# Layer 1 of a two-layer graph network with keys on partitions: eight accumulators, one exponential, row maxima by a fused instruction during layer 0

## The chip, the core and the metric

The kernel runs on one core of a Trainium2 chip. The metric is the device time of one execution in microseconds (us); each kernel is given as the median of its runs. A ratio is the mean time of one kernel's fast runs over that of the other's of the same rounds, so it is not quite the ratio of the medians quoted beside it.

In the profile PE is TensorE's matmul stream, PEld its weight loads, DVE is VectorE, ACT ScalarE, POOL GpSimd, SP the engine that issues DMAs. The granted clock is the share of its full clock that TensorE was given. L300 is line 300 of that kernel's file; the numbers shift between kernels, so I name tiles too.

## The reference, cut to what matters

```python
# x: (8, 2048, 256), adj: (2048, 2048) of 0 and 1, the same for all 8 batches
h = maximum(layernorm(x), 0)                     # layer 0: 4 heads, softmax per chunk of 256 keys
...                                              # scores clipped to +-10, masked, times v, projected,
x = x + layernorm(ctx @ Wo.T + bo + h) * gamma + beta
h = maximum(layernorm(x), 0) @ W                 # layer 1
e = leaky_relu((h @ a1)[:, :, None] + (h @ a2)[:, None, :], 0.01)
e = where(adj == 0, -1e9, e)
x = x + maximum(softmax(e) @ h, 0)               # over all 2048 keys
```

The logit of layer 1 is a function of a sum of two numbers, one of the query ("src", from a1) and one of the key ("dst", from a2).

## The kernel before

Eight batches one after the other. In layer 0 a batch has four blocks of 512 queries; each block has 16 passes (logits, mask, exponential, mix) for two heads and one chunk of keys, then a serial tail: output projection, two layer norms, and the start of layer 1.

The matmuls of this kernel write to PSUM (PE ps_s<-q,k and the like in the traces). I count it in tiles of 128x512 fp32 and call one a bank. The kernel uses eight of them, shared out as three rotating pools, each of two buffers:

```python
ps_s: [P, 2, 512]   # two banks each: logits of layer 0, transposes of layer 1
ps_a: [P, 512]      # mixes, accumulators of layer 1
ps_m: [P, 512]      # all small products and transposes
```

The start of layer 1 for a block, and layer 1 with queries on partitions:

```python
def start_layer1(x4, nb, sd):
    _, rn = norm_stats(x4)
    hT = normed_transposed(x4, rn)
    for t2 in range(TB // 2):
        pp = ps_m()
        ...  # matmul(pp, hT, w1s): layer 1's projection
        nc.scalar.activation(g[...], pp..., AF.Copy)
        ...  # four fused multiply-and-sum instructions on VectorE: src and dst into sd

def layer1(pool, b, xs, sd):
    ...  # dst spread over all partitions
    for t in range(NT):                                     # 16 tiles of queries
        nc.vector.scalar_tensor_tensor(d, sign[:, t, :], BIG, dst, op0=ALU.mult, op1=ALU.min)
        nc.vector.tensor_reduce(dmax, d, AX.X, ALU.max)     # both 128x2048
        ...
        for half in range(2):
            nc.scalar.activation(e1, d[:, cols], AF.Exp, bias=b1)
            nc.scalar.activation(e2, d[:, cols], AF.Exp, bias=b2, scale=SLOPE)
            nc.vector.tensor_tensor(e1, e1, e2, op=ALU.max)
            ...  # 8 transposes into ps_s, two evacuations, 8 matmuls into one accumulator
```

## Time and profile before

| | before |
|---|---|
| time | 5757.45 us (5756.26 to 5758.06, 3 runs) |
| layer 0 of a batch | 523.3 us |
| ends of layer 1's projection, from one block to the next | 116.3, 116.2, 104.1 us |
| layer 1 of a batch | 186.7 us |
| mean granted TensorE clock | 0.922 |

I use the same landmarks for every kernel. Layer 0 of a batch runs from the start of its first q projection to the end of layer 1's projection in its fourth block; layer 1 from there to the next batch's first q projection. They are read from TensorE's order of time, and are medians over the eight batches.

The windows of the first batch show the same stages (start and end; then length, and the busy time of PE, PEld, DVE, ACT and POOL, each with its count; then the granted clock, the DMA share and GB/s):

```profile
75.60:262.20 186.60, 184.57 (x970) 127.67 (x970) 88.61 (x180) 67.10 (x83) 37.03 (x43) 0.93 0.00 1
262.20:378.50 116.30, 114.55 (x691) 85.99 (x692) 67.01 (x142) 40.97 (x46) 32.12 (x37) 0.90 0.00 1
494.60:598.70 104.10, 84.76 (x563) 65.67 (x563) 56.98 (x133) 32.63 (x37) 30.22 (x34) 0.89 0.00 1
598.70:785.40 186.70, 152.38 (x793) 127.53 (x791) 152.24 (x231) 90.44 (x108) 20.08 (x19) 0.96 0.06 20
```

In the second block TensorE is busy 114.55 of 116.30 us, and in layer 1 TensorE and VectorE are busy 152 us each of 187.

### The profile page before, as it was taken

The numbers are of one execution on the slowest core, as the hardware profiler recorded it, in microseconds if no ns is written. First come the engines' busy times: TensorE is split into PE (matmuls) and PEld (weight loads), VectorE is DVE, ScalarE is ACT, GpSimd is POOL, SyncE is SP. The second block draws the span as 40 slices with busy tenths as digits, with TensorE's granted clock in tenths as the row PEclk, the third lists the DMA queues.
The fourth block names the chain that finished last, engine by engine and source line by source line (L and its number), as shares of the span: only waits on it lengthen the run. The fifth ranks groups of instructions, "written<-read, shape, count | busy, mean of one in ns | idle before, by whom it ended". The sixth has DMA issues, their size and how long they took to land.

```text
span 5753.9 us, 73951 instructions
## 1 busy us (share of the span) xinstructions
PE 5208.2 (91%) x29840; PEld 3939.6 (68%) x29840; DVE 3477.6 (60%) x6501; ACT 2191.4 (38%) x2545; POOL 1228.1 (21%) x1369
## 2 busy tenths in 40 slices
PE   7999799987999889998899978999789997899978
PEld 4777667766677666776667757676576776767767
DVE  4555755558455584555845558455584555845567
ACT  3333443334433344333533335433353333533334
POOL 2222102231022301223112221123211232112221
PEclk7999899999999899998999989999899988999889
DMA  4000000000000000000000000000000000000000
GB/s 150 1 1 1 15 15 1 1 1 15 15 1 1 1 15 15 1 1 1 19 11 1 1 1 23 8 1 1 1 23 8 1 1 1 23 4 1 1 1 15
DMA packets 39203, 57.16 MB, mean 10 GB/s; under 512 B 2000, under 2 KB 36816, under 8 KB 36816
## 3 DMA queue, kind: packets, MB, share of 16 engines
q1 hardware_dynamic: 38864, 52.44, 2.8%
q8 instruction: 238, 3.90, 0.3%
q14 instruction: 101, 0.83, 0.0%
HBM read 35.65 MB, written 16.78 MB: 9 GB/s over the span
## 4 chain that ended last, share of the span: by engine, by line
PE 74%; DVE 14%; POOL 6%; ACT 4%; issue 2%; DMA 0%; POOLq 0%; SPq 0%; ACTq 0%; DVEq 0%
PE ps_a L238 32%; PE ps_s L219 17%; PE ps_a L352 10%; PE ps_m L194 4%; DVE d L328 3%; PE ps_m L300 3%; DVE e L343 2%; DVE st L331 2%; PE ps_m L203 2%; PE ps_m L183 2%; PE ps_s L346 2%; POOL o L282 1%; DVE e L224 1%; PE ps_m L271 1%; ACT e L341 1%
## 5 line engine op out<-in xcount | busy, mean ns | idle before, releaser
L238 PEld LDWEIGHTS ps_a<-v,e 128*128 128x128 f32 x16384 | 1994.8, 202 | 357.8 <-issue 321.4
L238 PE MATMUL ps_a<-v,e 128*128 128x65 f32 x16384 | 2061.0, 287 | 0.0
L228 ACT ACTIVATE e<-e 128x1024 f32<-128x1024 f32 x1024 | 1081.8, 1056 | 1682.4 <-DVE e L224 1650.2
L224 DVE SCALAR_TENSOR_TENSOR e<-ps_s,bound 128x1024 f32<-128x1024 f32 x1024 | 1213.4, 1217 | 273.4 <-PE ps_s L219 273.2
L219 PE MATMUL ps_s<-q,k 64*128 64x512 f32 x4096 | 1211.3, 638 | 66.3 <-DVE e L224 66.3
L252 POOL TENSOR_TENSOR ctx<-ctx,part 128x256 f32<-128x256 f32 x896 | 648.0, 723 | 2698.9 <-DVE part L251 2698.9
L352 PE MATMUL ps_a<-g,eT 128*128 128x257 f32 x4096 | 952.9, 385 | 66.9 <-ACT eT L348 45.9
L352 PEld LDWEIGHTS ps_a<-g,eT 128*128 128x128 f32 x4096 | 756.7, 190 | 214.0 <-ACT eT L348 83.5
L219 PEld LDWEIGHTS ps_s<-q,k 64*128 64x128 f32 x4096 | 389.6, 190 | 391.2 <-issue 148.8
L243 DVE RECIPROCAL rz<-ps_a 128x4 f32<-128x4 f32 x1024 | 182.7, 180 | 783.3 <-PE ps_a L238 783.3
L346 PE MATMUL ps_s<-ident,e 128*128 128x128 f32 x2048 | 288.0, 282 | 180.7 <-DVE e L343 179.8
L251 DVE TENSOR_TENSOR part<-ps_a,rz 128x256 f32<-128x256 f32 x896 | 379.6, 424 | 88.5 <-DVE rz L243 1.4
L360 POOL TENSOR_TENSOR x<-x,r 128x256 f32<-128x256 f32 x128 | 136.3, 1065 | 1254.8 <-DVE st L332 511.9
L346 PEld LDWEIGHTS ps_s<-ident,e 128*128 128x128 f32 x2048 | 247.4, 145 | 221.7 <-DVE e L343 114.4
L348 ACT ACTIVATE eT<-ps_s 128x512 f32<-128x512 f32 x256 | 150.6, 590 | 615.8 <-PE ps_s L346 575.2
L343 DVE TENSOR_TENSOR e<-e,e 128x1024 f32<-128x1024 f32 x256 | 310.1, 1217 | 79.3 <-ACT e L342 79.3
L341 ACT ACTIVATE e<-d,st 128x1024 f32<-128x1024 f32 x256 | 291.2, 1137 | 112.8 <-DVE st L334 112.8
L328 DVE SCALAR_TENSOR_TENSOR d<-sign,dst 128x2048 f32<-128x2048 int8 x128 | 312.7, 2448 | 9.6 <-ACT dst L324 9.6
L342 ACT ACTIVATE e<-d,st 128x1024 f32<-128x1024 f32 x256 | 291.1, 1137 | 0.0
L331 DVE TENSOR_REDUCE st<-d 128x1 f32<-128x2048 f32 x128 | 290.5, 2274 | 0.0
L183 PE MATMUL ps_m<-ident,hn 128*128 128x128 f32 x512 | 121.0, 368 | 165.7 <-ACT hn L173 165.2
L183 PEld LDWEIGHTS ps_m<-ident,hn 128*128 128x128 f32 x512 | 67.2, 175 | 288.8 <-ACT hn L173 237.5
(71 smaller groups left out, 3130.3 us busy)
## 6 DMA issues: line engine op xcount, KB each, us to landing
rows<-in_adj_dram SPq DMA_DIRECT2D x16, 1024.0 KB, 5.0
x<-in_x_dram SPq DMA_DIRECT2D x32, 512.0 KB, 3.8
out_dram<-x SPq DMA_DIRECT2D x32, 512.0 KB, 2.9
raw<-in_L_gnn_Wq_dram SPq DMA_DIRECT2D x1, 256.0 KB, 4.7
raw<-in_L_gnn_Wk_dram SPq DMA_DIRECT2D x1, 256.0 KB, 4.9
raw<-in_L_gnn_Wv_dram SPq DMA_DIRECT2D x1, 256.0 KB, 5.3
raw<-in_L_gnn_Wo_dram SPq DMA_DIRECT2D x1, 256.0 KB, 5.1
w1s<-in_L_gnn_W_dram SPq DMA_DIRECT2D x1, 256.0 KB, 6.4
```

The lines of the kernel that those rows point to most:

```text
L219: nc.tensor.matmul(s[:, i, :], k[p][i * DH:(i + 1) * DH, mt * P:(mt + 1) * P], q[p][i * DH:(i + 1) * DH, cols], start=True, stop=True,)
L224: nc.vector.scalar_tensor_tensor(e, s, -CLIP * SC, bound[:, mt, cols][:, None, :].to_broadcast([P, 2, NB]), op0=ALU.max, op1=ALU.min,)
L228: nc.scalar.activation(e, e, AF.Exp, scale=1.0 / SC)
L238: nc.tensor.matmul(a[:, s, :], es[kt][:, i, t * P:(t + 1) * P], v[:, j * KT + kt, 2 * p + i, :], start=kt == 0, stop=kt == KT - 1,)
L251: nc.vector.tensor_tensor(part, num, rzb, op=ALU.mult)
L252: nc.gpsimd.tensor_tensor(dst, dst, part, op=ALU.add)
L328: nc.vector.scalar_tensor_tensor(d, sign[:, t, :], BIG, dst, op0=ALU.mult, op1=ALU.min)
L331: nc.vector.tensor_reduce(dmax, d, AX.X, ALU.max)
L341: nc.scalar.activation(e1, d[:, cols], AF.Exp, bias=b1)
L343: nc.vector.tensor_tensor(e1, e1, e2, op=ALU.max)
L346: nc.tensor.transpose(pt[:, k * P:(k + 1) * P], e1[:, k * P:(k + 1) * P], ident)
L352: nc.tensor.matmul(acc, eT[:, k * P:(k + 1) * P], g[:, m, :], start=m == 0, stop=m == NT - 1)
```

## The change

Its intent: in layer 1 keys go on partitions, so the exponentials are already in the layout that the matmul wants. The transposes and their evacuations fall away. The logit is rewritten so that one exponential does for two: with low = 0.01 dst and high = dst - low, leaky(src + dst) = Relu(0.99 src + high) + 0.01 src + low. The row's stabilising maximum needs the largest dst of a row's neighbours; that is computed block by block in layer 0 by a fused add-and-max on VectorE. All eight of these banks become accumulators for half of the queries at once.

The core of the diff (cuts marked with ...):

```diff
-    xpool = ctx.enter_context(tc.tile_pool(name="xpool", bufs=NNB + 1))
+    xpool = ctx.enter_context(tc.tile_pool(name="xpool", bufs=NNB))
...
-    w1s = const.tile([P, FC, F], F32, name="w1s")
+    w1s = const.tile([P, FC, F + 2], F32, name="w1s")      # W*a1, W*a2 as two more columns
...
         for t2 in range(TB // 2):
-            pp = ps_m()
+            pp = ps_s()
...
-            ...  # four fused multiply-and-sum instructions per pair of tiles
+            nc.vector.tensor_copy(sd[:, :, t0:t0 + 2]..., pp[:, :, F:F + 2])
+        far_d = work.tile([P, NB], F32, tag="far_d", name="far_d", bufs=1)
+        spread(far_d, sd[:, 1, nb * TB:(nb + 1) * TB], TINY)
+        for t in range(NT):
+            junk = work.tile([P, NB], BF16, tag="junk", name="junk", bufs=1)
+            nc.vector.tensor_tensor_reduce(
+                junk, far[:, t, nb * NB:(nb + 1) * NB], far_d, 1.0,
+                -2 * FAR if nb == 0 else dmax[:, t:t + 1], ALU.add, ALU.max, dmax[:, t:t + 1],
+            )
...
+        for half in range(N // W):
+            ...  # accs: 8 accumulators, 2 x ps_s of two banks, 2 x ps_a, 2 x ps_m
+            for m in range(NT):
+                e = pool.tile([P, W], F32, tag="e1", name="e1", bufs=5)
+                nc.scalar.activation(e, s_r[:, cols], AF.Relu, bias=high[:, m:m + 1], scale=1.0 - SLOPE)
+                nc.gpsimd.tensor_tensor(e, e, w_r[:, cols], op=ALU.add)
+                nc.scalar.activation(e, e, AF.Exp, bias=low[:, m:m + 1])
+                nc.vector.scalar_tensor_tensor(e, bound[:, m, cols], 0.0, e, op0=ALU.is_gt, op1=ALU.mult)
+                for k in range(W // P):
+                    nc.tensor.matmul(accs[k], e[:, k * P:(k + 1) * P], g[:, m, :], ...)
+            for k in range(W // P):
+                h1 = pool.tile([P, F + 1], F32, tag="h1", name="h1", bufs=2)
+                ...  # evacuate, divide, Relu on VectorE; add to x on GpSimd
```

More of the change, by code (lines that the diff above doesn't have):

```diff
@@ L23 @@
 SLOPE = 0.01
-BIG = 2.0 ** 36
+TINY = 2.0 ** -60
+FAR = 64.0
+NEVER = 1e30
 @with_exitstack
@@ L106, in gnn_two_layers @@
     woT = const.tile([P, FC, F], F32, name="woT")
-    w1s = const.tile([P, FC, F], F32, name="w1s")
+    w1s = const.tile([P, FC, F + 2], F32, name="w1s")
+    ones = const.tile([P, 1], F32, name="ones")
+    nc.gpsimd.memset(ones, 1.0)
     bound = const.tile([P, NT, N], I8, name="bound")
-    sign = const.tile([P, NT, N], I8, name="sign")
+    far = const.tile([P, NT, N], I8, name="sign")
     v = const.tile([P, NT, HEADS, DH + 1], F32, name="v")
@@ L134, in gnn_two_layers @@
             nc.vector.tensor_scalar(z, rows, 0.0, -2.0, op0=ALU.is_equal, op1=ALU.mult)
-            nc.gpsimd.tensor_scalar(sign[:, t, :], z, 1.0, 1.0, op0=ALU.mult, op1=ALU.add)
+            nc.gpsimd.tensor_scalar(far[:, t, :], z, FAR / 2, 0.0, op0=ALU.mult, op1=ALU.add)
             for half in range(NT // 8):
@@ L145, in gnn_two_layers @@
                     nc.scalar.activation(dst, pt, AF.Copy, bias=CLIP * SC, scale=CLIP * SC)
-    nc.sync.dma_start(w1s, w1.rearrange("(c p) f -> p c f", p=P))
+    nc.sync.dma_start(w1s[:, :, 0:F], w1.rearrange("(c p) f -> p c f", p=P))
     bo_r = row_bcast(bo, "bo_r")
@@ L152, in gnn_two_layers @@
     a2_r = row_bcast(a1[F:, 0], "a2_r")
+    for c in range(FC):
+        for i, a_r in enumerate((a1_r, a2_r)):
+            junk = work.tile([P, F], F32, tag="hn", name="junk", bufs=3)
+            nc.vector.scalar_tensor_tensor(
+                junk, w1s[:, c, 0:F], 1.0, a_r, op0=ALU.mult, op1=ALU.mult,
+                accum_out=w1s[:, c, F + i:F + i + 1],
+            )
     def norm_stats(t4, keep=False):
@@ L290, in finish_layer0, with start_layer1 @@
         nc.gpsimd.tensor_tensor(x4, x4, o4, op=ALU.add)
-    def start_layer1(x4, nb, sd):
+    def start_layer1(x4, nb, sd, dmax):
         _, rn = norm_stats(x4)
@@ L300, in start_layer1 @@
                     nc.tensor.matmul(
-                        pp[:, i * F:(i + 1) * F], hT[:, di, t * P:(t + 1) * P], w1s[:, di, :],
+                        pp[:, i, 0:F + 2], hT[:, di, t * P:(t + 1) * P], w1s[:, di, :],
                         start=di == 0, stop=di == FC - 1,
@@ L304, in start_layer1, with spread @@
             t0 = nb * TB + 2 * t2
-            nc.scalar.activation(g[:, t0:t0 + 2, 0:F], pp.rearrange("p (i f) -> p i f", i=2), AF.Copy)
-            for t in (t0, t0 + 1):
-                for i, a_r in enumerate((a1_r, a2_r)):
-                    junk = work.tile([P, F], F32, tag="hn", name="junk", bufs=3)
-                    nc.vector.scalar_tensor_tensor(
-                        junk, g[:, t, 0:F], 1.0, a_r, op0=ALU.mult, op1=ALU.mult,
-                        accum_out=sd[:, i, t:t + 1],
-                    )
-    def layer1(pool, b, xs, sd):
-        HALF = N // 2
-        dst = pool.tile([P, N], F32, tag="dst", name="dst", bufs=1)
-        for c4 in range(NT // 4):
+            nc.scalar.activation(g[:, t0:t0 + 2, 0:F], pp[:, :, 0:F], AF.Copy)
+            nc.vector.tensor_copy(
+                sd[:, :, t0:t0 + 2].rearrange("p s t -> p t s"), pp[:, :, F:F + 2]
+            )
+        far_d = work.tile([P, NB], F32, tag="far_d", name="far_d", bufs=1)
[5 more added lines that the diff above has]
+                -2 * FAR if nb == 0 else dmax[:, t:t + 1], ALU.add, ALU.max, dmax[:, t:t + 1],
+            )
+    def spread(dst, col, scale=1.0):
+        for c4 in range(col.shape[1] // 4):
             pt = ps_m()
@@ L321, in layer1 @@
                 nc.tensor.transpose(
-                    pt[:, i * P:(i + 1) * P], sd[:, 1, t:t + 1].to_broadcast([P, P]), ident
+                    pt[:, i * P:(i + 1) * P], col[:, t:t + 1].to_broadcast([P, P]), ident
                 )
-            nc.scalar.activation(dst[:, c4 * 512:(c4 + 1) * 512], pt, AF.Copy)
-        for t in range(NT):
-            src = sd[:, 0, t:t + 1]
-            d = pool.tile([P, N], F32, tag="d", name="d", bufs=2)
-            nc.vector.scalar_tensor_tensor(d, sign[:, t, :], BIG, dst, op0=ALU.mult, op1=ALU.min)
-            st = small.tile([P, 5], F32, tag="st", name="st")
-            zmax, top, b1, b2, dmax = (st[:, i:i + 1] for i in range(5))
-            nc.vector.tensor_reduce(dmax, d, AX.X, ALU.max)
-            nc.vector.tensor_tensor(zmax, dmax, src, op=ALU.add)
-            nc.vector.scalar_tensor_tensor(top, zmax, SLOPE, zmax, op0=ALU.mult, op1=ALU.max)
-            nc.vector.tensor_tensor(b1, src, top, op=ALU.subtract)
-            nc.vector.scalar_tensor_tensor(b2, src, SLOPE, top, op0=ALU.mult, op1=ALU.subtract)
-            acc = ps_a()[:, 0:F + 1]
-            for half in range(2):
-                cols = slice(half * HALF, (half + 1) * HALF)
-                e1 = pool.tile([P, HALF], F32, tag="e1", name="e1", bufs=3)
-                e2 = pool.tile([P, HALF], F32, tag="e2", name="e2", bufs=3)
-                nc.scalar.activation(e1, d[:, cols], AF.Exp, bias=b1)
-                nc.scalar.activation(e2, d[:, cols], AF.Exp, bias=b2, scale=SLOPE)
-                nc.vector.tensor_tensor(e1, e1, e2, op=ALU.max)
-                pt = ps_s().rearrange("p a n -> p (a n)")
-                for k in range(8):
-                    nc.tensor.transpose(pt[:, k * P:(k + 1) * P], e1[:, k * P:(k + 1) * P], ident)
-                eT = pool.tile([P, HALF], F32, tag="eT", name="eT", bufs=2)
-                nc.scalar.activation(eT[:, 0:512], pt[:, 0:512], AF.Copy)
-                nc.vector.tensor_copy(eT[:, 512:], pt[:, 512:])
-                for k in range(8):
-                    m = half * 8 + k
@@ new lines, in spread, with layer1 @@
+            nc.scalar.activation(dst[:, c4 * 512:(c4 + 1) * 512], pt, AF.Copy, scale=scale)
+    def layer1(pool, b, xs, sd, dmax):
+        W = N // 2
+        src, dst = sd[:, 0, :], sd[:, 1, :]
+        s_r = pool.tile([P, N], F32, tag="s_r", name="s_r", bufs=1)
+        spread(s_r, src)
+        top = pool.tile([P, 3, NT], F32, tag="top", name="top", bufs=1)
+        none, w, zm = (top[:, i, :] for i in range(3))
+        part = pool.tile([P, 2, NT], F32, tag="part1", name="part1", bufs=1)
+        low, high = part[:, 0, :], part[:, 1, :]
+        nc.vector.tensor_scalar(low, dst, SLOPE, None, op0=ALU.mult)
+        nc.vector.tensor_tensor(high, dst, low, op=ALU.subtract)
+        w_r = pool.tile([P, N], F32, tag="w_r", name="w_r", bufs=1)
+        nc.vector.tensor_scalar(none, dmax, -FAR / 2, None, op0=ALU.is_lt)
+        nc.vector.scalar_tensor_tensor(zm, dmax, 1.0 / TINY, src, op0=ALU.mult, op1=ALU.add)
+        nc.vector.scalar_tensor_tensor(zm, zm, SLOPE, zm, op0=ALU.mult, op1=ALU.max)
+        nc.vector.scalar_tensor_tensor(w, src, SLOPE, zm, op0=ALU.mult, op1=ALU.subtract)
+        nc.vector.scalar_tensor_tensor(w, none, -NEVER, w, op0=ALU.mult, op1=ALU.add)
+        spread(w_r, w)
+        pg = ps_m()
+        for m in range(NT):
+            nc.tensor.matmul(
+                pg[:, 0:F + 1], ones.to_broadcast([P, P]), g[:, m, :], start=m == 0, stop=m == NT - 1
+            )
+        gsum = pool.tile([P, F + 1], F32, tag="gsum", name="gsum", bufs=1)
+        nc.scalar.activation(gsum, pg[:, 0:F + 1], AF.Copy)
+        for half in range(N // W):
+            cols = slice(half * W, (half + 1) * W)
+            accs = []
+            for _ in range(2):
+                two = ps_s()
+                accs += [two[:, 0, 0:F + 1], two[:, 1, 0:F + 1]]
+            accs += [ps_a()[:, 0:F + 1] for _ in range(2)] + [ps_m()[:, 0:F + 1] for _ in range(2)]
+            for m in range(NT):
+                e = pool.tile([P, W], F32, tag="e1", name="e1", bufs=5)
+                nc.scalar.activation(
+                    e, s_r[:, cols], AF.Relu, bias=high[:, m:m + 1], scale=1.0 - SLOPE
+                )
+                nc.gpsimd.tensor_tensor(e, e, w_r[:, cols], op=ALU.add)
+                nc.scalar.activation(e, e, AF.Exp, bias=low[:, m:m + 1])
+                nc.vector.scalar_tensor_tensor(
+                    e, bound[:, m, cols], 0.0, e, op0=ALU.is_gt, op1=ALU.mult
+                )
+                for k in range(W // P):
@@ L352, in layer1 @@
                     nc.tensor.matmul(
-                        acc, eT[:, k * P:(k + 1) * P], g[:, m, :], start=m == 0, stop=m == NT - 1
+                        accs[k], e[:, k * P:(k + 1) * P], g[:, m, :], start=m == 0, stop=m == NT - 1
                     )
-            rz = small.tile([P, 1], F32, tag="rz1", name="rz1")
-            nc.vector.reciprocal(rz, acc[:, F:F + 1])
-            r = work.tile([P, F], F32, tag="hn", name="r", bufs=3)
-            nc.vector.tensor_scalar(r, acc[:, 0:F], rz, 0.0, op0=ALU.mult, op1=ALU.max)
@@ L359, in layer1 @@
-            x4 = xs[t // TB]
-            nc.gpsimd.tensor_tensor(x4[:, t % TB, :], x4[:, t % TB, :], r, op=ALU.add)
-            if t % TB == TB - 1:
-                nb = t // TB
-                nc.sync.dma_start(
-                    out[b, nb * NB:(nb + 1) * NB, :].rearrange("(t p) f -> p t f", p=P), x4
-                )
+            for k in range(W // P):
+                t = half * (W // P) + k
+                h1 = pool.tile([P, F + 1], F32, tag="h1", name="h1", bufs=2)
+                nc.vector.scalar_tensor_tensor(
+                    h1, gsum, none[:, t:t + 1], accs[k], op0=ALU.mult, op1=ALU.add
+                )
+                rz = small.tile([P, 1], F32, tag="rz1", name="rz1")
+                nc.vector.reciprocal(rz, h1[:, F:F + 1])
+                nc.vector.tensor_scalar(h1[:, 0:F], h1[:, 0:F], rz, 0.0, op0=ALU.mult, op1=ALU.max)
+                x4 = xs[t // TB]
+                nc.gpsimd.tensor_tensor(x4[:, t % TB, :], x4[:, t % TB, :], h1[:, 0:F], op=ALU.add)
+                if t % TB == TB - 1:
+                    nb = t // TB
+                    nc.sync.dma_start(
+                        out[b, nb * NB:(nb + 1) * NB, :].rearrange("(t p) f -> p t f", p=P), x4
+                    )
@@ L368, in gnn_two_layers @@
     for b in range(B):
         sd = small.tile([P, 2, NT], F32, tag="sd", name="sd", bufs=2)
+        dmax = small.tile([P, NT], F32, tag="dmax", name="dmax", bufs=2)
         with tc.tile_pool(name="l0", bufs=1, reuse_waits="tile") as pool:
@@ L390, in gnn_two_layers @@
                 finish_layer0(pool, xs[nb], rns[nb], ctx4)
-                start_layer1(xs[nb], nb, sd)
+                start_layer1(xs[nb], nb, sd, dmax)
         with tc.tile_pool(name="l1", bufs=1, reuse_waits="tile") as pool:
-            layer1(pool, b, xs, sd)
+            layer1(pool, b, xs, sd, dmax)
 _INS = [
```

## The prediction

> **What bounds the kernel now.** I read the page first, then the order of time stage by stage, because a share over the whole span mixes two layers. TensorE leads:
>
> ```profile
> PE 5208.2 (91%) x29840; PEld 3939.6 (68%) x29840; DVE 3477.6 (60%) x6501; ACT 2191.4 (38%) x2545; POOL 1228.1 (21%) x1369
> PE 74%; DVE 14%; POOL 6%; ACT 4%; issue 2%; DMA 0%; POOLq 0%; SPq 0%; ACTq 0%; DVEq 0%
> ```
>
> Busy time, then the chain that ended last: TensorE carries 74% of it. TensorE in order of time inside a block of layer 0 (start, duration, group):
>
> ```profile
> 273.41 1.99 PE L219 MATMUL ps_s<-q,k 64*128 64x512 f32 x8
> 275.33 3.79 PE L238 MATMUL ps_a<-v,e 128*128 128x65 f32 x32
> 279.05 1.99 PE L219 MATMUL ps_s<-q,k 64*128 64x512 f32 x8
> ```
>
> One pass (logits, then mix, for two heads and one chunk) takes 279.05 - 273.41 = 5.64 us without a gap; a block of 512 queries has 16. At a block's end stands a serial chain (output projection, two layer norms, GpSimd adds, transposes, layer 1's projection). At the end of a batch's first block TensorE hides it under the next block:
>
> ```profile
> 224.15 1.99 PE L271 MATMUL ps_m<-woT,cT 128*128 128x256 f32 x8
> 226.07 1.99 PE L219 MATMUL ps_s<-q,k 64*128 64x512 f32 x8
> ...
> 246.26 1.68 PE L183 MATMUL ps_m<-ident,hn 128*128 128x128 f32 x6 [0.24 <-ACT hn L173]
> ```
>
> Between the output projection (L271) and the transposes (L183) it runs the next block's logits and mixes. After the fourth block there is no next block, and the bare chain shows:
>
> ```profile
> 570.01 1.99 PE L271 MATMUL ps_m<-woT,cT 128*128 128x256 f32 x8 [0.69 <-ACT cT L267]
> 589.41 2.16 PE L183 MATMUL ps_m<-ident,hn 128*128 128x128 f32 x8 [17.40 <-ACT hn L173]
> 592.14 6.58 PE L300 MATMUL ps_m<-w1s,hT 128*128 128x256 f32 x16 [0.57 <-DVE hT L184]
> ```
>
> 17.4 us idle, then a slow projection (6.58 us for 16, against 4.97 at the second block). Keep this in mind: it decides the prediction.
>
> Layer 1 then runs from 598.72 to the next batch's first projection at 785.41: 186.7 us. Its windows show TensorE and VectorE both near full (103 and 105 busy of 115 us from 620), ScalarE at half.
>
> The costs of what comes in:
>
> ```profile
> L289 POOL TENSOR_TENSOR o<-o,beta_r 128x1024 f32<-128x1024 f32 x32 | 75.3, 2352 | 2.5
> L341 ACT ACTIVATE e<-d,st 128x1024 f32<-128x1024 f32 x256 | 291.2, 1137 | 112.8 <-DVE st L334 112.8
> L309 DVE SCALAR_TENSOR_TENSOR junk<-g,a_r 128x256 f32<-128x256 f32 x256 | 93.6, 421 | 124.3 <-ACT g L305 124.3
> L309 DVE DVE_READ_ACCUMULATOR junk<-g,a_r 128x1 f32 x256 | 21.0, 82 | 0.0
> ```
>
> A GpSimd addition of 128x1024 takes 2.35 us, an activation of 128x1024 with a bias column 1.14 us, a fused multiply and row sum of 128x256 0.42 us plus its accumulator read.
>
> [...]
> - [...] the 17.4 us above pass with nothing pulled in. [...]
> - [...]
>
> ```profile
> 740.32 1.22 DVE L343 TENSOR_TENSOR e<-e,e 128x1024 f32<-128x1024 f32 x1
> 740.48 1.64 POOL L360 TENSOR_TENSOR x<-x,r 128x256 f32<-128x256 f32 x1 [7.18 <-DVE r L358]
> 741.45 2.82 DVE L328 SCALAR_TENSOR_TENSOR d<-sign,dst 128x2048 f32<-128x2048 int8 x1
> ```
>
> The GpSimd addition, 0.72 us alone, took 1.64; the VectorE instruction behind it 2.82 instead of 2.28.
> - [...] the trace's 2.35 is used.
> - [...]
>
> **The change: layer 1.** Out go, per batch, 256 transposes, their evacuations, one of two exponentials, and the 16 wide masks and row maxima. In come 32 stages (2 halves of queries, 16 key tiles): Relu on ScalarE, addition on GpSimd, Exp on ScalarE, mask on VectorE, 8 matmuls (16 instructions of 0.209 us, at the spacing of L352: 3.34 us). If TensorE bounded them: 32 x 3.34 = 107 us.
>
> But the built program's order on ScalarE is, in the steady state, Relu n, Exp n, Relu n+1, Exp n+1. Exp n needs the addition n, which needs Relu n; so ScalarE stands still during GpSimd's work and the five buffers don't help. A stage is then 1.14 (Relu) + 2.35 (addition) + 1.04 (Exp, to the next start) + about 0.1 for hand-overs [...]: 4.7 us, and TensorE waits.
>
> From T, the end of layer 1's projection in the fourth block:
> - copies and transposes to the first row maximum 2.2 us (0.6 us each, as L321 and L324 show); [...] five small column operations 1.0; transposes and copies of w 2.0: T+17.
> - the first five stages have their Relu done [...]: the sixth Relu starts at T+34. Ten more starts and the second half's first: 11 x 4.7 = T+86.
> - five stages of the second half, 23.5. VectorE's order puts three of their masks ahead of the eight accumulators of the first half, so TensorE gets its banks late and the first buffer comes free some 4.5 us late: T+114. The next two stages run as a pair in 7, nine more 42.3: T+163.5.
> - last mask 1.3; the eight evacuations overlap the last matmuls, and the banks that the next batch's transposes need come last, about T+172.5; transposes and copy 3.2: T+175.7.
>
> Against 186.7 that gains 11 us a batch.
>
> **The change: layer 0.** The projection of layer 1 now takes its PSUM tile from the logits' pair of buffers. The next block's logits are allocated after it and must follow it. The order of the built program shows it on TensorE: output projection, 8 transposes, projection, transposes for the maxima, and only then the next block's logits. The bare chain is exposed in all four blocks. From the last mix's end (565.8) to 598.72 it takes 32.9 us.
>
> After it, VectorE has the 16 maxima interleaved with the first masks[...]. Counting down its order, the fourth pass's exponentials are ready at 27 us and its mix ends at 31; then 12 passes of 5.64, the last without logits (-1.9): 96.8. With 32.9 a block takes 129.7 us, three 389. The first block's last mix would end at about 217, its projection at 250 instead of 262.2 (257.07 + 5.15). Layer 0's end, now 598.7, comes at 250 + 389 = 639: **40 us later** per batch. (Before, the blocks' projections end 116.2, 116.2 and 104.1 us apart: the first ones pay little for the chain.)
>
> **The sum.** +40 - 11 = +29 us a batch, 8 batches: +232 on 5757, 5990 us with setup's four extra products.
>
> **Rivals.**
> - *The intent holds*: stages at TensorE's 3.34 us, chain hidden. 32 x 1.36 = 44 us a batch more, and no loss in layer 0: 5757 - 8 x 55 = about 5320. For it: the work on every engine falls. Against it: both orders, on ScalarE and TensorE.
> - *Only layer 1's part counts*: the exposed chain replaces waits that exist already. 5670. For it: the blocks' ends are not free now (116.2 against 16 x 5.64 + about 10 of other work). I counted that, by working from blocks' whole periods.
> - *The row maximum is slow* [...] No such instruction is in this trace[...].
> - *TensorE's clock*: after each exposed gap it may stay slow longer (mixes of 6.93 instead of 3.79 us stand at 250.35). Up to 4 us a block, about 6090.
>
> **Range and chances.** The exposed chain is read from the program's order and an identical stretch of the trace, so its sign is firm; its size could be off by 10 us a batch, and layer 1 by as much. Combined, about 110 us either way: 5880 to 6110. Within 2% (under 5872) needs both to be wrong in the same direction: 0.12. Faster needs the order not to matter: 0.04. Slower: 0.84.
>
> **What would show it.** Right: idle of about 17 us ahead of the block-end transposes 32 times instead of 8; starts of Relu 4.7 us apart in layer 1, with ScalarE waiting for GpSimd; [...] layer 0 about 640 us in the first batch. Wrong: blocks still 116 us apart, or stages near 3.4 us with TensorE busy throughout.

Some of this text is cut, at the marks: statements of how the hardware behaves that no trace or run of this study shows, with the terms that rested on them. The results are as recorded: +40 us a batch in layer 0 and -11 in layer 1, so +29 a batch, +232 in all, 5990 us. Terms of that sum are cut, so it can't be added up from what is left:

- T+17 had a term for the 16 row maxima; the terms that stand are 2.2 + 1.0 + 2.0 = 5.2 us. An estimate from the trace alone: an addition of 128x512, one input in PSUM, took VectorE 0.68 us on average in the kernel before (L275), and an accumulator read 0.08 (L309), and 16 x 0.76 = 12.2, which gives T+17.4. The 27 and 31 us in layer 0 contain the same cut figure.
- A stage's 4.7 us: the terms that stand come to 1.14 + 2.35 + 1.04 + 0.1 = 4.63; a small one is cut.
- T+34: what one of the first five stages takes is cut, and the pair in 7 us rests on the same thought. An estimate from the trace: an addition and a mask one after the other, 2.35 + 1.22 = 3.57 us. It gives T+35. The signs of it in the kernel before are printed above: an addition that began beside a VectorE instruction took 1.64 us instead of 0.72, and the VectorE instruction that began beside it 2.82 instead of 2.28.

That TensorE keeps to its program order was an assumption of mine; the trace above shows only 17.4 us with nothing pulled in. before_shared_psum below fits it: with one line of the order changed, the waits before the transposes rise from 165.2 us in all to 563.7. The 3.34 us of a stage's matmuls doesn't fit the trace: four matmuls of L352 in a row, from 640.16 us on, took 1.03 us and one alone takes 0.38, so they start 0.217 us apart and not 0.209.

## The result and the profile after

The changed kernel takes 5952.57 us (5951.31 to 5953.0, 4 runs) against 5756.85 us of the kernel before beside it: ratio 1.034 (95% interval 1.0325 to 1.0355). It is slower, by 196 us or 24.5 us a batch.

| per batch, us | before | after | difference | predicted difference |
|---|---|---|---|---|
| layer 0 | 523.3 | 553.1 | +29.8 | +40 |
| layer 1 | 186.7 | 180.7 | -6.0 | -11 |

Busy time and the chain that ended last, from the page of the changed kernel:

```profile
PE 4897.3 (82%) x28304; PEld 3684.2 (62%) x28304; DVE 3133.4 (53%) x6245; ACT 2116.9 (36%) x2361; POOL 1837.6 (31%) x1626
PE 56%; POOL 16%; DVE 14%; issue 8%; ACT 6%; DMA 0%; POOLq 0%; SPq 0%; ACTq 0%; DVEq 0%
```

Three of the engines do less work than before, and the kernel is slower. TensorE's share of the chain fell from 74% to 56%, and GpSimd's rose from 6% to 16%: time went from work to waits. Two windows of the first batch, its second block and layer 1:

```profile
251.80:377.70 125.90, 105.71 (x694) 79.52 (x692) 74.27 (x157) 41.45 (x46) 32.74 (x37) 0.92 0.00 1
630.90:811.50 180.60, 135.99 (x589) 111.19 (x587) 84.93 (x141) 79.58 (x82) 93.16 (x50) 0.89 0.05 17
```

The second block now lasts 125.90 us with TensorE busy 105.71; before it lasted 116.30 with 114.55. In layer 1 no engine is near full.

TensorE in order of time at the end of the first block, where the kernel before had the next block's passes:

```profile
224.28 1.99 PE L283 MATMUL ps_m<-woT,cT 128*128 128x256 f32 x8 [0.69 <-ACT cT L279]
243.28 2.16 PE L195 MATMUL ps_m<-ident,hn 128*128 128x128 f32 x8 [17.00 <-ACT hn L185]
246.02 5.76 PE L312 MATMUL ps_s<-w1s,hT 128*128 128x258 f32 x16 [0.57 <-DVE hT L196]
```

Output projection, 17.00 us of nothing, transposes, projection: the bare chain, now in the first block too. Over the whole span the list of waits has it, in us in total, times and the longest, first of the kernel before, then of the changed one:

```profile
PE ps_m L183 <- ACT hn L173: 165.2, 32, 17.4
```

```profile
PE ps_m L195 <- ACT hn L185: 551.5, 40, 17.3
```

At 17 us each, eight full waits (139 of the 165.2) have become 32 (some 543 of the 551.5). The fused row maxima, with their accumulator's first value from a column (blocks 1 to 3) and without (block 0); busy time and mean in ns come after the bar:

```profile
L326 DVE CUSTOM_DVE_ANT_0 junk<-sign,far_d,dmax 128x512 bf16<-128x512 int8 x384 | 292.3, 761 | 33.7 <-ACT far_d L340 29.4
L326 DVE CUSTOM_DVE_ANT_0 junk<-sign,far_d 128x512 bf16<-128x512 int8 x128 | 90.7, 709 | 11.7 <-ACT far_d L340 11.7
```

And a steady stage of layer 1, in order of time (Relu is L379, the addition L382, Exp L383):

```profile
676.43 1.13 ACT L379 ACTIVATE e<-s_r,part 128x1024 f32<-128x1024 f32 x1
...
677.64 2.35 POOL L382 TENSOR_TENSOR e<-e,w_r 128x1024 f32<-128x1024 f32 x1 [2.30 <-ACT e L379]
...
680.02 1.15 ACT L383 ACTIVATE e<-e,part 128x1024 f32<-128x1024 f32 x1 [2.46 <-POOL e L382]
681.07 1.13 ACT L379 ACTIVATE e<-s_r,part 128x1024 f32<-128x1024 f32 x1
```

From Relu to Relu 681.07 - 676.43 = 4.64 us. ScalarE and GpSimd take turns: each stands still while the other works on the same tile.

### The profile page after: what moved, and what is told of

It is laid out like the page before. It is cut to its first block, busy times and chain, and to the rows that moved or that the text cites. A ratio compares the mean times of both kernels' runs of the same rounds, so it can differ in the third digit from the quotient of the medians.

```text
span 5951.2 us, 70683 instructions
## 1 busy us (share of the span) xinstructions
PE 4897.3 (82%) x28304; PEld 3684.2 (62%) x28304; DVE 3133.4 (53%) x6245; ACT 2116.9 (36%) x2361; POOL 1837.6 (31%) x1626
## 4 chain that ended last, share of the span: by engine, by line
PE 56%; POOL 16%; DVE 14%; issue 8%; ACT 6%; DMA 0%; POOLq 0%; SPq 0%; ACTq 0%; DVEq 0%
PE ps_a L250 27%; PE ps_s L231 14%; POOL e L382 9%; DVE junk L326 4%; PE ps_m L206 4%; ACT e L379 3%; DVE e L236 3%; PE ps_s L312 2%; PE ps_m L283 2%; PE ps_m L215 2%; PE ps_m L195 1%; DVE e L384 1%; POOL x L302 1%; POOL o L301 1%; POOL o L300 1%
## 5 line engine op out<-in xcount | busy, mean ns | idle before, releaser
L382 POOL TENSOR_TENSOR e<-e,w_r 128x1024 f32<-128x1024 f32 x256 | 635.6, 2489 | 671.4 <-ACT e L379 449.4
L384 DVE SCALAR_TENSOR_TENSOR e<-bound,e 128x1024 f32<-128x1024 int8 x256 | 374.7, 1464 | 672.6 <-ACT e L383 667.3
L388 PE MATMUL ps_s<-g,e 128*128 128x257 f32 x2048 | 533.4, 405 | 154.8 <-DVE h L394 100.1
L195 PE MATMUL ps_m<-ident,hn 128*128 128x128 f32 x512 | 121.4, 384 | 588.5 <-ACT hn L185 551.5
L388 PEld LDWEIGHTS ps_s<-g,e 128*128 128x128 f32 x2048 | 405.3, 202 | 252.2 <-DVE h L394 109.1
L383 ACT ACTIVATE e<-e,part 128x1024 f32<-128x1024 f32 x256 | 293.9, 1148 | 583.0 <-POOL e L382 583.0
L326 DVE CUSTOM_DVE_ANT_0 junk<-sign,far_d,dmax 128x512 bf16<-128x512 int8 x384 | 292.3, 761 | 33.7 <-ACT far_d L340 29.4
L379 ACT ACTIVATE e<-s_r,part 128x1024 f32<-128x1024 f32 x256 | 287.5, 1136 | 61.2 <-PE ps_m L388 61.2
L388 PE MATMUL ps_m<-g,e 128*128 128x257 f32 x1024 | 271.7, 387 | 40.5 <-ACT gsum L369 38.7
L388 PE MATMUL ps_a<-g,e 128*128 128x257 f32 x1024 | 268.2, 383 | 7.1 <-DVE h L394 7.1
L388 PEld LDWEIGHTS ps_m<-g,e 128*128 128x128 f32 x1024 | 194.2, 192 | 75.7 <-ACT gsum L369 41.9
```

Of the source, the lines that this page charges most:

```text
L326: nc.vector.tensor_tensor_reduce(junk, far[:, t, nb * NB:(nb + 1) * NB], far_d, 1.0, -2 * FAR if nb == 0 else dmax[:, t:t + 1], ALU.add, A ...
L379: nc.scalar.activation(e, s_r[:, cols], AF.Relu, bias=high[:, m:m + 1], scale=1.0 - SLOPE)
L382: nc.gpsimd.tensor_tensor(e, e, w_r[:, cols], op=ALU.add)
L383: nc.scalar.activation(e, e, AF.Exp, bias=low[:, m:m + 1])
L384: nc.vector.scalar_tensor_tensor(e, bound[:, m, cols], 0.0, e, op0=ALU.is_gt, op1=ALU.mult)
L388: nc.tensor.matmul(accs[k], e[:, k * P:(k + 1) * P], g[:, m, :], start=m == 0, stop=m == NT - 1)
```

## The experiments

My theory after reading this: the tail of each block is exposed because layer 1's projection takes its PSUM tile from the logits' pool; layer 1 gains little because ScalarE's order puts each Exp right behind the addition it waits for; and the maxima cost 16 x 0.79 us ahead of layer 1. The rival: these waits lie beside something else, so that taking them away gives nothing. Nine kernels ran beside the kernel before, in three groups on three chips (four, four and then one_maximum); the record holds four times of each, also of h8, for which five rounds instead of three were asked. The kernel before took 5757.52, 5757.84 and 5757.57 us in the three groups, so I compare across them. All gave results judged correct, also the ones that no longer compute the same function in general.

| run | time, us | ratio to before | layer 0 | layer 1 |
|---|---|---|---|---|
| changed kernel | 5952.57 | 1.0340 | 553.1 | 180.7 |
| before_shared_psum | 5920.48 | 1.0285 | 543.8 | 186.6 |
| proj_own_psum | 5965.17 | 1.0361 | 556.7 | 180.6 |
| no_maxima | 5760.72 | 1.0006 | 542.1 | 167.9 |
| relu_ahead | 5787.33 | 1.0053 | 554.0 | 159.4 |
| own_psum_no_maxima | 5599.80 | 0.9725 | 523.1 | 166.4 |
| own_psum_paced_maxima | 5787.26 | 1.0050 | 532.6 | 180.8 |
| paced_relu_ahead_h8 | 5546.43 | 0.9632 | 530.3 | 152.3 |
| h8 | 5926.17 | 1.0292 | 553.8 | 176.7 |
| one_maximum | 5480.57 | 0.9520 | 530.6 | 141.8 |

### before_shared_psum: the suspected pool, in the kernel before

```diff
         for t2 in range(TB // 2):
-            pp = ps_m()
+            pp = ps_s()[:, 0, :]
```

> The kernel before with one edit: layer 1's projection takes its PSUM tile from the logits' pair; no maxima, old layer 1. Theory A: the chain is exposed in all four blocks, the first batch's layer 0 ends some 25 us later than 598.7, and the time rises from 5757 to about 5955 us (5920 to 6000). Theory B: nothing of VectorE's work has changed, so 5757 within 20 us.

It took 5920.48 us (interval of the ratio 1.0267 to 1.0302), at the lower edge of theory A's range. One line of the old kernel costs 163 us, 20.5 a batch, and nothing in layer 1 moves (186.6 against 186.7). The exposed tail is thereby shown as a cause by itself. Each of the three tails that had been hidden costs 20.5 / 3 = 6.8 us, which is much less than the 17 us of idle time that appear.

Why so little? First two windows of the kernel before, in the stretch in which it hides a tail under the next block's passes (226 to 262), then the second block of before_shared_psum:

```profile
238.00:258.00 20.00, 19.76 (x71) 14.59 (x71) 8.22 (x22) 5.74 (x8) 5.79 (x6) 0.50 0.00 1
254.00:258.00 4.00, 4.00 (x18) 3.85 (x18) 0.73 (x4) 0.00 (x0) 0.72 (x1) 0.50 0.00 0
```

```profile
243.00:366.00 123.00, 102.67 (x689) 78.28 (x688) 68.01 (x139) 41.08 (x45) 32.18 (x37) 0.92 0.00 1
```

In the kernel before TensorE is busy 19.76 of 20 us there, at half the clock. The overlap that I had taken for free runs at about half speed: the 32 matmuls of a mix took 6.93 us at 250.35, and 3.79 at 275.33. With the tail exposed, the second block's matmuls keep TensorE busy 102.67 us where the kernel before needed 114.55: of some 18.6 us of added idle time 11.9 come back, which leaves 6.7. Why the clock falls in the hidden tail isn't tested.

### proj_own_psum: the projection back in the small pool, in the changed kernel

```diff
-        for t2 in range(TB // 2):
-            pp = ps_s()
+        for t in range(TB):
+            pp = ps_m()[:, 0:F + 2]
```

> The changed kernel with layer 1's projection put back into the pair of one-bank PSUM tiles, one tile of 258 columns at a time; everything else of the change stays. Theory A (the loss in layer 0 is the block-end chain, exposed because the projection shares the logits' PSUM tiles): the 17 us idle ahead of the block-end transposes is left 8 times instead of 32, layer 0 of the first batch ends near 600 us instead of 631, and the time falls by 8 x 30 to about 5710 us (5680 to 5740). Theory B (the loss is VectorE, slowed by the row maxima): blocks stay 126 us apart and the time stays within 20 us of 5953.

It took 5965.17 us (5960.85 to 5969.63), 13 us more than the changed kernel: 255 us off theory A's number and inside theory B's (though the blocks came about 123 us apart, not theory B's 126). Read by the time alone, it refutes the exposed tail as a cause, against what the other kernel showed. But the order of time shows the next block's passes back inside the tail, the full waits of about 17 us are down from 32 to 8, and TensorE's busy share rose from 82% to 89%. So the edit did what it was to do, and something took the gain. The windows after the second block of the first batch, where the 16 maxima now fall beside full passes (columns as above; DVE's busy time is the third):

```profile
400.00:405.00 5.00, 4.32 (x30) 2.98 (x30) 5.00 (x14) 2.12 (x2) 1.17 (x1) 1.00 0.00 0
405.00:410.00 5.00, 4.34 (x31) 3.07 (x30) 5.00 (x12) 1.65 (x2) 1.17 (x1) 1.00 0.00 0
415.00:430.00 15.00, 15.00 (x57) 11.71 (x58) 4.27 (x8) 2.11 (x2) 2.02 (x4) 0.50 0.00 0
```

First VectorE is full, 5.00 of 5.00 us: the masks of the passes queue behind the maxima, and TensorE waits in small pieces (0.68, 0.49 and 0.76 us before three of its groups, each until VectorE). Then its clock is halved while VectorE has little to do. Over the span the mean clock fell to 0.888 from the changed kernel's 0.910. That was an observation in search of a test, and it made a new theory: the two costs hide each other. With the tail exposed, TensorE has nothing to do anyway when the maxima come; with the tail hidden, the burst of maxima stops it.

### no_maxima and own_psum_no_maxima: the maxima out, with each of the two pools

```diff
-        far_d = work.tile(...)
-        spread(far_d, ...)
-        for t in range(NT):
-            ...  # the 16 fused maxima
+        if nb == 0:
+            nc.vector.memset(dmax, 0.0)
```

With the maxima go their inputs, the spread of dst over the partitions and its four transposes a block, so the two runs price both together. Both are another function in general: with zero for the largest neighbour's term, a row with large terms could overflow and a row without a neighbour isn't noticed.

> The changed kernel without the 64 row maxima of a batch and their transposes, the maxima set to 0 (result may be wrong for a row without a neighbour; on purpose). Theory A: the chain stays exposed (17 us idle 32 times); the blocks come 2 to 4 us closer, and layer 1 starts 13 us earlier: 5953 - 8 x (13 + 9) = about 5780 us (5750 to 5820). Theory B: blocks return to 116 us, so 8 x (13 + 32) less, about 5595 us.

> The changed kernel with both edits at once: the projection of layer 1 in the small pool as in the kernel before, and no row maxima (zero in their place; not the same function in general). Each alone gave: projection back 5965, maxima out 5761, the change 5953. Theory A (the two costs hide each other: with the chain overlapped, TensorE has masks to wait for, and the burst of 16 maxima on VectorE stalls it and halves its granted clock, so the overlap only pays once the maxima are out): layer 0 is back near the 523 us per batch of the kernel before, plus some 4 for the wider projection and the spread, layer 1 near the 168 of the run without maxima, 695 in place of 710: 5640 (5600 to 5690). Theory B (overlapping the chain is worth nothing with the new start of layer 1, whatever the maxima do): as without maxima alone, 5760 (within 20).

They took 5760.72 us and 5599.80 us; the first is inside theory A's range, the second 0.2 us below its own. With the two runs that have the maxima this makes a square:

| us | projection in the logits' pool | in the small pool | gain of the small pool |
|---|---|---|---|
| with maxima | 5952.57 | 5965.17 | -13 |
| without | 5760.72 | 5599.80 | 161 |
| gain without maxima | 192 | 365 | |

Theory A of the second run holds: the overlap is worth 161 us, near the 163 of the kernel before, but only without the burst; and the burst with its spread costs 365 us where TensorE would have had work, 192 where it hadn't. No sum of separate costs could have said this. How much of the 365 is the bunching, the next run shows. Layer 0 is back at 523.1 us, the old kernel's 523.3. Of the 192, layer 1 has 12.8 us a batch (from the projection's end to its first accumulation it took 15.2 us instead of 26.4) and layer 0 11.0.

### own_psum_paced_maxima: the same maxima, spread out

```diff
+    def row_maxima(far_d, nb, dmax, some, beside=None):
+        for t in some:
+            junk = beside.tile([P, NB], BF16, tag="part", name="junk", bufs=3)   # the mixes' own rotation
...
                 for n, (p, j) in enumerate(todo):
+                    if nb > 0 and n >= 4:
+                        row_maxima(far_d, nb - 1, dmax, range(4 * (n - 4) // 3, 4 * (n - 3) // 3), pool)
```

Issuing them between the passes in the program was not enough, by my reading of a built order that no run on record has (so it is not shown): they were still bunched at the front, because they were ready. Sharing a rotating buffer with the mixes' quotients, which gets a third buffer for it, ties each to its pass. The projection is in the small pool here; the last block's maxima stay in one bunch ahead of layer 1.

> All maxima kept, projection in the small pool, but the 16 maxima of blocks 0 to 2 are spread over passes 4 to 15 of the next block (their output shares a rotating buffer with the quotients of the mixes, so the scheduler cannot bunch them); those of the last block stay where they are. Theory A (the burst is what costs, not the work: one or two maxima of 0.76 us fit into the 2 us that VectorE idles in each pass of 5.63): layer 0 near 528 us per batch, layer 1 near the changed kernel's 181, 5750 (5710 to 5790). Theory B (the work itself costs wherever it is, or the overlap is worth nothing): near the 5965 of the projection alone, at least 5900.

It took 5787.26 us, 178 us less than with the burst and inside theory A's range, near its upper end. VectorE and TensorE in order of time in a pass with one maximum:

```profile
306.91 0.68 DVE L328 CUSTOM_DVE_ANT_0 junk<-sign,far_d 128x512 bf16<-128x512 int8 x1
307.52 0.08 DVE L328 DVE_READ_ACCUMULATOR2_ANT dmax<- 128x1 f32 x1
307.52 2.35 DVE L236 SCALAR_TENSOR_TENSOR e<-ps_s,bound 128x1024 f32<-128x1024 f32 x2
```

```profile
306.24 1.99 PE L231 MATMUL ps_s<-q,k 64*128 64x512 f32 x8
311.88 1.99 PE L231 MATMUL ps_s<-q,k 64*128 64x512 f32 x8
```

The pass is 311.88 - 306.24 = 5.64 us, as in the kernel before. So 178 of the 365 us were the bunching in the first three blocks: layer 0 fell by 24.1 us a batch, layer 1 not at all. The rest is what still lies ahead of layer 1 (it takes 180.8 us, against 166.4 without maxima) and layer 0's 532.6 us, where 528 was expected and own_psum_no_maxima has 523.1; one_maximum below says something on that.

### relu_ahead: ScalarE two stages ahead

```diff
+                r = pool.tile([P, W], F32, tag="r1", name="r1", bufs=3)
-                nc.scalar.activation(e, s_r[:, cols], AF.Relu, ...)
-                nc.gpsimd.tensor_tensor(e, e, w_r[:, cols], op=ALU.add)
-                nc.scalar.activation(e, e, AF.Exp, bias=low[:, m:m + 1])
+                nc.scalar.activation(r, s_r[:, cols], AF.Relu, ...)
+                nc.gpsimd.tensor_tensor(r, r, w_r[:, cols], op=ALU.add)
+                e = pool.tile([P, W], F32, tag="e1", name="e1", bufs=5)
+                nc.scalar.activation(e, r, AF.Exp, bias=low[:, m:m + 1])
```

> The changed kernel with the Relu's output in buffers of its own (3), so that the order on ScalarE becomes Relu n+2 ahead of Exp n; the same instructions otherwise. Theory A (a stage is the chain Relu, GpSimd addition, Exp in ScalarE's order): a stage falls from 4.65 us [...], layer 1 of a batch falls by about 25 us, and the time to about 5745 us (5700 to 5790). Rival (GpSimd and VectorE together, or TensorE after its idle gaps, bound the stage already): the stage stays above 4.3 us and the time within 60 us of 5953.

As an estimate from the traces, an addition (2.35) and a mask (1.22) one after the other are about 3.6 us.

It took 5787.33 us, 165 us less than the changed kernel, at the upper part of the range. Layer 1 fell by 21.3 us a batch and layer 0 stayed (554.0). TensorE's first groups of two successive stages:

```profile
673.74 1.90 PE L389 MATMUL ps_s<-g,e 128*128 128x257 f32 x8
...
677.20 1.90 PE L389 MATMUL ps_s<-g,e 128*128 128x257 f32 x8
```

A stage is now 677.20 - 673.74 = 3.46 us, and TensorE has no gap in it: it bounds the stage. The order on ScalarE was the cause of the 4.64. The next bound is close: GpSimd is now busy without a pause, twelve additions in 39.61 us (from 662.06 us on) or 3.30 each, beside the masks on VectorE, where an addition alone takes 2.35.

### h8: eight buffers for the finished rows

```diff
-                h1 = pool.tile([P, F + 1], F32, tag="h1", name="h1", bufs=2)
+                h1 = pool.tile([P, F + 1], F32, tag="h1", name="h1", bufs=8)
```

> The changed kernel with one number changed: eight buffers for the normalised rows of layer 1 in place of two. Theory A (the last evacuations are paced at 2.5 us a pair by GpSimd's additions, which give the two buffers back, and those of the half boundary likewise, and both are on the path to the next TensorE work): some 3 to 5 us per batch, 5920 (5905 to 5935). Theory B (what follows waits for something else, the input or the last additions): 5950 (within 8).

It took 5926.17 us, 26 us less than the changed kernel; layer 1 fell by 4.0 us a batch. In the changed kernel the last evacuations come in pairs 2.5 us apart, each pair after GpSimd's additions:

```profile
805.13 0.48 DVE L394 SCALAR_TENSOR_TENSOR h<-gsum,top,ps_a 128x257 f32<-128x257 f32 x1 [0.61 <-POOL x L401]
...
807.63 0.48 DVE L394 SCALAR_TENSOR_TENSOR h<-gsum,top,ps_m 128x257 f32<-128x257 f32 x1 [0.61 <-POOL x L401]
808.26 1.51 PE L195 MATMUL ps_m<-ident,hn 128*128 128x128 f32 x6 [5.29 <-DVE h L394]
```

The next batch's transposes wait for the last banks. With eight buffers VectorE doesn't wait for GpSimd there, and from the last accumulation's end to the next batch's projection it takes 5.3 us instead of 8.5.

### paced_relu_ahead_h8: the three mends together

> The run above with the additions of layer 1 two stages ahead (the Relu in a tile of its own, three of them) and eight buffers for the normalised rows in place of two. If the three costs add up (20 us per batch of overlap regained, 21 of the stage's chain, 3 to 5 of the evacuations), layer 0 takes 528 and layer 1 some 156 per batch: 5550 (5510 to 5600), faster than both kernels. If the gains overlap as those of the first runs did: 5600 to 5700.

It took 5546.43 us, ratio 0.9632 (0.9618 to 0.9647). It computes the same function as the changed kernel and beats both. Layer 0 takes 530.3 us and layer 1 152.3. The gains more than add up: on top of the paced maxima the two edits gave 241 us, alone they had given 165 and 26. Part of the surplus is at the half boundary of layer 1, where TensorE's longest wait is 2.8 us; it was 5.7 with relu_ahead alone and 11.0 with h8 alone.

### one_maximum: one maximum for the batch instead of one per row

```diff
-            ...  # row_maxima and its calls
+        nc.vector.tensor_reduce(dmax[:, nb:nb + 1], far_d, axis=AX.X, op=ALU.max)
...
-        nc.vector.scalar_tensor_tensor(zm, dmax, 1.0 / TINY, src, op0=ALU.mult, op1=ALU.add)
+        nc.vector.tensor_reduce(d_top[:, 0:1], dmax[:, 0:NNB], axis=AX.X, op=ALU.max)
+        nc.vector.tensor_scalar(zm, src, d_top[:, 0:1], None, op0=ALU.add)
```

> The fastest run so far (paced maxima, Relu ahead, eight buffers; 5546) with the sixteen row maxima per block replaced by one maximum of the block's terms, so that all rows share the largest term of the batch; which rows have no neighbour is found once, at the start. It guards against overflow as before, but not against a row whose own terms all lie far below the batch's largest, so it is a weaker function on other data. Theory A (the maxima are all that separates layer 0 from the kernel before, 530 against 523 us per batch, and 11 of the 26 us ahead of layer 1's first accumulation): 18 to 20 us per batch, 5395 (5370 to 5430). Theory B (with the maxima out another wait takes their place, the transposes of the source terms or the small steps): less than 10 us per batch, above 5465.

It took 5480.57 us, 66 us less than the run above or 8.2 a batch: near theory B's number, but not for theory B's reason. Layer 1 gained the 10.5 us that I expected of it. Layer 0 didn't move (530.6 against 530.3), so the paced maxima had cost it no more than the one maximum per block in their place. And finding the rows without a neighbour at the start made the start longer: the first q projection begins at 95.1 us instead of 77.9. The sum is 8 x 10.2 - 17.2 = 64 us. What keeps layer 0 some 7 us above own_psum_no_maxima should then come with what the two still differ in there, the spread of dst over the partitions and what follows from it. Part of it shows as clock: in the first batch's third block TensorE is busy 117.24 us at a granted clock of 0.89 in paced_relu_ahead_h8 (372 to 491 us), and 110.55 us at 0.93 in own_psum_no_maxima (375 to 491). No run has the spread alone; the cause stays open.

## Why the prediction was right, and where its numbers were off

The call, slower by over 2%, and its main reason stood. That the total, 5990 us, came within 38 us is partly luck: layer 0's loss was put 10 us a batch too high and layer 1's gain 5 us too high, and the two errors partly cancel. By its own steps:

- **Layer 0: the chain bare in all four blocks.** Right, and shown by before_shared_psum in the other kernel. The size was 29.8 us instead of 40. The mis-sized term is the block's 129.7 us; it measured 126.4 (from 251.78 to 630.86 in three blocks). Of the 3.3 us, 2.7 are the ramp: the fourth mix ended 28.3 us after the projection, at 280.1, not 31. Another 1.2 are the chain: from the last mix's end at 220.1 to 251.8 it took 31.7, not 32.9, mostly as the projection took 5.76 us and not 6.58. The passes after the fourth mix gave 0.6 back.
- **What I had not split.** The term mixed two causes. The exposed chain alone is 20.5 us a batch (before_shared_psum), and the other 9 come with the maxima and their spread (layer 0 loses 11.0 us when they go). The prediction counted the maxima inside the ramp and never asked what they would do where there was no ramp. That is why my first experiment's expectation, 5710, missed by 255 us.
- **The row maxima.** Measured were 0.71 us without a first value and 0.76 with one, and before layer 1 they follow each other at 0.79 us, 12.6 us for 16. The rival of a slow maximum is out: they are close to the 0.68 us of an addition of 128x512 in the kernel before (L275).
- **Layer 1's stage.** 4.7 us predicted, 4.64 measured; relu_ahead confirms the cause. The bound behind it, which I put at 3.34 us a stage, is 3.46 in relu_ahead.
- **Layer 1's ends.** It gains 6.0 us a batch instead of 11. The banks came free 177.4 us after the projection, not 172.5. The terms: the sixth Relu started 35.7 us after the projection, not 34, and the second half's first Relu at 87.4, not 86; the second half's first free buffer took 30.0 us from its first Relu, not 28, and the last evacuations were paced at 2.5 us a pair by the two buffers. I had counted the evacuations without GpSimd; h8 returns 4.0 us a batch.
- **The rivals.** The intent, 5320, is not reached by any run (5480.57 is the least, and it has no maximum per row); layer 1 with TensorE as its bound exists (relu_ahead, 159.4 us), but with 11 us of maxima ahead of it. "Only layer 1's part counts", 5670, is answered by before_shared_psum: the chain alone costs 163 us. TensorE's clock after the exposed gap cost no more than before: in the changed kernel it is 0.50 from 230 to 250 us, but back at 0.99 in the window from 250 to 254 us, so earlier than in the kernel before, where it is still 0.50 from 254 to 258.

## What to carry to other kernels

When an independent later stage lies behind a tile of its own pool in TensorE's program order, sharing that pool with a late product serialised the two here (before_shared_psum: 163 us); check the built order for every tile that changes pools. Two costs that fall into the same gap can't be priced one by one: take each away with and without the other, as four runs. Work that "fits beside" a busy engine's helper by its total must also fit by its placing: 12 us of maxima in one bunch cost what the same maxima at one or two a pass did not (5965.17 us in proj_own_psum, 5787.26 in own_psum_paced_maxima).

## What the traces show of the clock and of two instructions

- **When the clock fell.** In the changed kernel's 17.00 us gap, up to 243.28 us, the clock was 0.95 from 226 to 230 us and 0.50 from 230 on. In proj_own_psum it was 1.00 until 410 us, 0.90 from 410 to 415 and 0.50 from 415 on, after 10 us in which TensorE was busy 4.3 of each 5 us, and no gap there was longer than 0.76 us. So it fell in one long gap, and also after many small ones. How much idle time in small pieces is enough, no run shows.
- **When it came back.** In the kernel before it stayed at 0.50 through windows from 238 to 258 us in which TensorE was busy 19.76 of 20 us, and in proj_own_psum from 415 to 430 us with TensorE busy 15 of 15. So a TensorE that the trace shows busy throughout, or nearly, stayed at half clock for 20 and 15 us.
- **The fused maximum.** For 128x512 a median of 0.68 us without a first value from a column and 0.75 with one (means 0.71 and 0.76; some took 1.09), plus 0.08 for the accumulator's read, and 0.79 us from one to the next.
- **GpSimd's addition.** Undisturbed additions of 128x1024 took 2.35 us; beside the masks of relu_ahead 3.30 each.
